# A residual block's 3x3 convolutions, from two output rows at a time to four

## Chip, cores and metric

The program runs on one core of one Trainium2 chip. The metric is the device time of one execution in microseconds (us), the median of several runs. A core has TensorE (PE, matrix products into PSUM), VectorE (DVE), ScalarE (ACT), GpSimd (POOL) and SyncE (SP, which here only issues DMA transfers). Each engine takes its instructions in its own order; semaphores tie the engines together.

## What is computed

An image tensor x of shape 2 x 128 x 128 x 128 (batch B, channels, rows H, columns), float32, runs through four layers. Layers 0 and 2 are a 3x3 convolution with a small state-space scan over eight tokens, group norm and SiLU; layer 1 scales by a coarse gate. The change is in layer 3, a residual block with binarised weights:

```python
w1b = w1 + lax.stop_gradient(jnp.sign(w1) - w1)
w2b = w2 + lax.stop_gradient(jnp.sign(w2) - w2)
out = jax.nn.relu(_batchnorm(_conv3x3(x, w1b), gamma1, beta1))
out = _batchnorm(_conv3x3(out, w2b), gamma2, beta2)
out = out + x
return jax.nn.relu(out)
```

Batch norm takes mean and variance over batch, rows and columns, so the second convolution starts only when the first is complete.

## The kernel before

Channels lie on the 128 partitions. Layers 0 to 2 take the program to about 6937 us. The function `_basic_block` is layer 3. Its whole result Y (2 x 128 rows of 128 columns, 128 KiB a partition) stays in SBUF; the block works in 32 bands of `BAND` = 8 rows, 16 to an image.

Both convolutions use a Winograd form along the rows: a pair of output rows is had from four input rows. Four combinations of input rows (the four lines of `combine`, L855, on POOL) are each multiplied by one of four combinations of the three weight rows (`u`, made once at the start, L817 to L827), for the three columns of the kernel (`kw`), so that a band of four pairs takes 4 x 3 = 12 matmuls of 512 columns (L862) into a PSUM tile `m` of four banks. There are two such tiles. ACT copies one product to SBUF (L870), DVE makes the even and odd rows from the four products by four additions (L873 to L876), and two `bn_stats` (L878) take the band's statistics.

`convolve` runs over the bands with `tc.manual_schedule`, so each engine keeps the order in which the code is written: in step k the load of band k+3, the making of band k+2, the combinations of band k+1, and matmuls and emptying (`conv`) of band k. In the first convolution `load` (L915, L917) fetches y and the residual, `residual` applies group norm and SiLU on ACT (L923), adds the residual on POOL (L924) and stores the band to x3 in DRAM (L925). In the second `normalised` copies two rows from the band before on POOL (L936) and applies batch norm and ReLU on ACT (L938). Three band buffers and two buffers for the combinations turn round. After the second convolution a last loop (L949 to L952) loads x3, adds, applies ReLU and stores the output.

Of the kernel before, what the change touches and what calls it, by code (L numbers as in the profile page):

```python
# [24 lines left out]
F32 = mybir.dt.float32  # L25
U8 = mybir.dt.uint8
AF = mybir.ActivationFunctionType
ALU = mybir.AluOpType
# [3 lines left out]
P = 128  # L32
# [10 lines left out]
BAND = 8  # L43
# [748 lines left out]
                        stage(*order[n - lag])  # L792


def _basic_block(tc, src, y, norm, x3, w1, w2, bn, out, B, H):

    nc = tc.nc  # L800
    pairs = BAND // 2
    with tc.tile_pool(name="bb", bufs=1) as cp, tc.tile_pool(name="bband", bufs=2) as bp, tc.tile_pool(
        name="ps_c", bufs=2, space=PSUM
    ) as pp:

        def combined():
            return bp.tile([P, 4, pairs, P + 2], F32, tag="comb", name="comb")

        bnc = cp.tile([P, 4], F32, tag="bnc", name="bnc")
        nc.sync.dma_start(out=bnc, in_=bn)  # L810
        ws = []
        for n, wd in enumerate((w1, w2)):
            room = [combined().rearrange("p a b c -> p (a b c)")[:, : 9 * P] for _ in range(2)]
            wt, sg = room
            nc.sync.dma_start(out=wt, in_=wd)
            nc.scalar.activation(sg, wt, AF.Sign)
            nc.vector.tensor_tensor(sg, sg, wt, ALU.subtract)  # L817
            nc.vector.tensor_tensor(wt, wt, sg, ALU.add)

            u = cp.tile([P, 4, 3, P], F32, tag=f"u{n}", name=f"u{n}")  # L820
            g = wt.rearrange("p (k t c) -> p k t c", k=3, t=3)
            half = sg.rearrange("p (k t c) -> p k t c", k=3, t=3)
            nc.vector.tensor_copy(u[:, 0:4:3], g[:, 0:3:2])
            nc.vector.tensor_tensor(half[:, 0], g[:, 0], g[:, 2], ALU.add)
            nc.vector.tensor_tensor(u[:, 1], half[:, 0], g[:, 1], ALU.add)
            nc.vector.tensor_tensor(u[:, 2], half[:, 0], g[:, 1], ALU.subtract)
            nc.vector.tensor_scalar_mul(u[:, 1:3], u[:, 1:3], 0.5)  # L827
            ws.append(u)
        Y = cp.tile([P, B, H, P], F32, tag="Y", name="Y")

        room = []
        for n in range(3):
            room.append(cp.tile([P, BAND + 2, P + 2], F32, tag=f"band{n}", name="band"))
            nc.gpsimd.memset(room[n][:, :, 0 : P + 2 : P + 1], 0.0)
        bands = [(b, r0) for b in range(B) for r0 in range(0, H, BAND)]

        def span(k):

            r0 = bands[k][1]
            return room[k % 3], 1 if r0 == 0 else 0, BAND + 1 if r0 + BAND == H else BAND + 2  # L840

        def border(k):
            xb, lo, hi = span(k)
            if lo == 1:
                nc.gpsimd.memset(xb[:, 0, :], 0.0)
            if hi == BAND + 1:
                nc.gpsimd.memset(xb[:, BAND + 1, :], 0.0)

        def combine(k):

            xb = span(k)[0]
            v = combined()
            d = [xb[:, n : n + BAND - 1 : 2, :] for n in range(4)]
            for i, (m, n, op) in enumerate(((0, 2, ALU.subtract), (1, 2, ALU.add), (2, 1, ALU.subtract), (1, 3, ALU.subtract))):
                nc.gpsimd.tensor_tensor(v[:, i], d[m], d[n], op)  # L855
            return v

        def conv(u, v, b, r0, stats):
            m = pp.tile([P, 4, pairs, P], F32, tag="m", name="m")
            for i in (1, 2, 0, 3):  # L860
                for kw in range(3):
                    nc.tensor.matmul(  # L862
                        m[:, i],
                        lhsT=u[:, i, kw, :],
                        rhs=v[:, i, :, kw : kw + P],
                        start=(kw == 0),
                        stop=(kw == 2),
                    )
            m1 = bp.tile([P, pairs, P], F32, tag="m1", name="m1")
            nc.scalar.copy(m1, m[:, 1])  # L870
            rows = Y[:, b, r0 : r0 + BAND, :]
            y0, y1 = rows[:, 0:BAND:2, :], rows[:, 1:BAND:2, :]
            nc.vector.tensor_tensor(y0, m1, m[:, 2], ALU.add)  # L873
            nc.vector.tensor_tensor(y1, m1, m[:, 2], ALU.subtract)
            nc.vector.tensor_tensor(y0, y0, m[:, 0], ALU.add)
            nc.vector.tensor_tensor(y1, y1, m[:, 3], ALU.subtract)  # L876
            for n in range(BAND // ROWS):
                nc.vector.bn_stats(  # L878
                    stats[:, (b * H + r0) // ROWS + n, :],
                    rows[:, n * ROWS : (n + 1) * ROWS, :].rearrange("p r w -> p (r w)"),  # L880
                )

        def affine(stats, n):
            mv = cp.tile([P, 2], F32, tag=f"mv{n}", name="mv")
            nc.vector.bn_aggr(mv, stats.rearrange("p a b -> p (a b)"))
            rstd = _rstd(nc, cp, mv[:, 1:2], BN_EPS, f"bn{n}")
            return _affine(nc, cp, mv[:, 0:1], rstd, bnc[:, 2 * n : 2 * n + 1], bnc[:, 2 * n + 1 : 2 * n + 2], f"bn{n}")

        def rest():
            return bp.tile([P, BAND + 2, P], F32, tag="xs", name="xs")  # L890

        def convolve(u, load, make, n):

            stats = cp.tile([P, B * H // ROWS, 6], F32, tag="st", name="st")
            v = {}
            E = mybir.EngineType
            with tc.manual_schedule(engines={E.PE, E.Activation, E.DVE, E.Pool, E.SP}):
                for k in range(-3, len(bands)):
                    for ahead, f in ((3, load), (2, make)):
                        if 0 <= k + ahead < len(bands):  # L900
                            f(k + ahead)
                    if 0 <= k + 1 < len(bands):
                        v[k + 1] = combine(k + 1)
                    if k >= 0:
                        conv(u, v.pop(k), *bands[k], stats)
            return affine(stats, n)

        rests = {}

        def load(k):  # L910
            b, r0 = bands[k]
            xb, lo, hi = span(k)
            rows = slice(r0 - 1 + lo, r0 - 1 + hi)
            border(k)
            nc.sync.dma_start(out=xb[:, lo:hi, 1 : P + 1], in_=y[b][:, rows, :])  # L915
            rests[k] = rest()[:, lo:hi, :]
            nc.sync.dma_start(out=rests[k], in_=src[b][:, rows, :])  # L917

        def residual(k):
            b, r0 = bands[k]  # L920
            xb, lo, hi = span(k)
            x = xb[:, lo:hi, 1 : P + 1]
            nc.scalar.activation(x, x, AF.Silu, bias=norm[b][1], scale=norm[b][0])  # L923
            nc.gpsimd.tensor_tensor(x, x, rests.pop(k), ALU.add)  # L924
            nc.sync.dma_start(out=x3[b][:, r0 : r0 + BAND, :], in_=xb[:, 1 : BAND + 1, 1 : P + 1])  # L925

        s1, t1 = convolve(ws[0], load, residual, 0)

        def normalised(k):
            b, r0 = bands[k]
            hb, lo, hi = span(k)
            border(k)
            if lo == 0:
                nc.gpsimd.tensor_copy(hb[:, 0:2, 1 : P + 1], span(k - 1)[0][:, BAND : BAND + 2, 1 : P + 1])  # L936
                lo = 2
            nc.scalar.activation(  # L938
                hb[:, lo:hi, 1 : P + 1], Y[:, b, r0 + lo - 1 : r0 + hi - 1, :], AF.Relu, bias=t1, scale=s1
            )  # L940

        s2, t2 = convolve(ws[1], lambda k: None, normalised, 1)

        for k, (b, r0) in enumerate(bands):
            if k % 2 == 0:
                xr = rest()[:, :BAND, :]
            else:
                xr = combined().rearrange("p a b c -> p (a b c)")[:, : BAND * P].rearrange("p (r w) -> p r w", r=BAND)
            nc.sync.dma_start(out=xr, in_=x3[b][:, r0 : r0 + BAND, :])  # L949
            nc.vector.scalar_tensor_tensor(xr, Y[:, b, r0 : r0 + BAND, :], s2, xr, ALU.mult, ALU.add)  # L950
            nc.scalar.activation(xr, xr, AF.Relu, bias=t2)
            nc.scalar.dma_start(out=out[b, :, r0 : r0 + BAND, :], in_=xr)  # L952
# [3 lines left out]
def _program(ctx, tc, d, cols, out):  # L956
    nc = tc.nc
    B, _, H, _ = d["x"].shape
# [5 lines left out]
    with tc.tile_pool(name="const", bufs=1) as cp, tc.tile_pool(name="wts", bufs=1) as wp:  # L964
# [4 lines left out]
        w1 = cp.tile([P, CG], F32, tag="w1", name="w1")  # L969
# [18 lines left out]
        w, stats = layer(x2, 2)  # L988
        with tc.tile_pool(name="ps_n", bufs=1, space=PSUM) as pp:
            norm = [_norm(nc, npool, pp, w, con, stats, b) for b in range(B)]  # L990
    _basic_block(tc, x2, y, norm, x3, d["L3_w1"], d["L3_w2"], d["L3_bn"], out, B, H)


def _host_layout(inputs):
# [40 lines left out]
```

## Time and profile before

| | us |
|---|---|
| median of 3 runs | 7748.62 (7738.88 to 7761.49) |
| span of the profiled run | 7761.8 |
| block begins (first load of its weights) | 6937.5 |
| first convolution, first to last matmul | 6970.5 to 7302.4 |
| second convolution, first to last matmul | 7315.1 to 7647.0 |
| last loop, to the end | 7647.0 to 7761.8 |

A profile page lists, for one execution, the busy time of each engine, groups of equal instructions by source line with count, mean duration and the idle time of the engine just before them (with what ended it), and the chain of work that ended last. A timeline gives the start and length of each instruction, and a table by stage the busy time of each engine in a stretch of time with the TensorE clock granted in it (1.00 is full speed). One float32 matmul appears as two matmul records, each with a weight load (PEld) of its own. The end of a matmul is modelled, so records that follow each other overlap. Of the whole span DVE is busy 6759.3 us and PE 6470.4 us; the earlier layers make up most of both.

### The profile page before, as it was taken

What the parts mean: (1) busy time and instruction counts of PE and PEld (TensorE: products, weight loads), DVE (VectorE), ACT (ScalarE), POOL (GpSimd) and SP (SyncE); (2) the same over time, 40 slices, a digit from 0 to 9 for tenths busy, and PEclk for the clock granted to TensorE, in tenths of its full rate; (3) what the DMA queues carried; (4) which work ended last, traced back from release to release, by engine and by line L of the source; (5) the groups of instructions that cost most, each with busy time, mean ns of one, the idle gap of its engine ahead of it and who ended that gap; (6) DMA issues with size and microseconds to landing.
All of it is one profiled execution on the core that took longest, in us unless ns stands there. A gap on an engine that the chain in (4) does not pass through costs nothing.

```text
span 7761.8 us, 87240 instructions
## 1 busy us (share of the span) xinstructions
PE 6470.4 (83%) x29648; PEld 2196.5 (28%) x29648; DVE 6759.3 (87%) x6304; ACT 4272.3 (55%) x4873; POOL 5628.0 (73%) x1879
## 2 busy tenths in 40 slices
PE   7888888888888888867888888888888888869994
PEld 2222222222222222243222222222222222224441
DVE  5999999999999999965999999999999999983333
ACT  4666665665666666554566565665666666631112
POOL 5777877877877778742777777777777777767541
PEclk8999999999999999877999999999999999979997
DMA  7999999999999999954999999999999999975204
GB/s 194 248 252 247 254 245 247 249 251 250 253 244 254 248 247 253 240 185 137 238 249 250 247 247 246 253 252 244 250 253 247 252 246 251 250 202 173 93 0 168
DMA packets 573438, 1767.29 MB, mean 228 GB/s; under 512 B 85536, under 2 KB 239680, under 8 KB 458176
## 3 DMA queue, kind: packets, MB, share of 16 engines
q1 hardware_dynamic: 568384, 1744.92, 86.3%
q10 hardware_dynamic: 4608, 16.78, 0.5%
q8 instruction: 236, 3.87, 0.2%
q14 instruction: 210, 1.72, 0.1%
HBM read 1551.65 MB, written 209.72 MB: 227 GB/s over the span
## 4 chain that ended last, share of the span: by engine, by line
DVE 35%; DMA 31%; PE 19%; issue 6%; POOL 4%; ACT 4%; SPq 2%; POOLq 0%; DVEq 0%; ACTq 0%
DMA bcr<-sb 24%; DVE set L471 12%; DVE h L476 10%; DVE r L472 10%; PE m L862 9%; DMA ur<-su 3%; POOL h L444 3%; PE one L348 2%; PE set L453 2%; ACT set L462 1%; PE one L399 1%; PE ys L491 1%; DVE v L504 1%; PE ys L482 1%; DMA band<-in_x_dram 1%
## 5 line engine op out<-in xcount | busy, mean ns | idle before, releaser
L444 POOL TENSOR_TENSOR h<-ur,bcr 128x2048 f32<-128x2048 f32 x896 | 4059.3, 4537 | 1282.1 <-DMA bcr<-sb 1063.4
L471 DVE TENSOR_TENSOR set<-set,h 128x1024 f32<-128x1024 f32 x1792 | 2192.2, 1223 | 297.3 <-ACT set L462 291.8
L472 DVE TENSOR_TENSOR r<-set,bcr 128x1024 f32<-128x1024 f32 x1792 | 2193.8, 1224 | 61.4
L462 ACT ACTIVATE set<-set 128x1024 f32<-128x1024 f32 x1792 | 1745.2, 1007 | 843.2 <-PE set L453 828.6
L476 DVE TENSOR_TENSOR h<-set,h 128x1024 f32<-128x1024 f32 x1536 | 1862.7, 1213 | 38.8 <-POOL h L444 38.3
L453 PE MATMUL set<-dt,rep 32*128 32x512 f32 x7168 | 1402.4, 674 | 95.9 <-DVE h L476 90.3
L491 PE MATMUL ys<-r,ct 128*32 128x512 f32 x7168 | 1165.6, 633 | 32.2 <-DVE r L472 32.0
L321 PE MATMUL one<-band,conv 128*128 128x512 f32 x2304 | 1086.6, 608 | 23.3 <-DMA band<-in_x_dram 12.6
L399 PE MATMUL one<-xc,keep 128*64 128x512 f32 x1024 | 319.6, 707 | 476.4 <-ACT xc L356 361.4
L862 PE MATMUL m<-comb,u 128*128 128x512 f32 x1536 | 663.8, 595 | 38.7 <-POOL comb L855 38.7
L453 PEld LDWEIGHTS set<-dt,rep 32*128 32x128 f32 x7168 | 407.4, 193 | 988.3 <-issue 468.3
L321 PEld LDWEIGHTS one<-band,conv 128*128 128x128 f32 x2304 | 408.7, 190 | 674.1 <-issue 599.5
L482 PE MATMUL ys<-t,ct 128*128 128x512 f32 x512 | 325.4, 722 | 251.3 <-DVE v L504 249.8
L350 ACT ACTIVATE xc<-one,keep 128x512 f32<-128x512 f32 x256 | 176.0, 687 | 516.6 <-PE one L348 511.9
L491 PEld LDWEIGHTS ys<-r,ct 128*32 128x32 f32 x7168 | 182.5, 111 | 916.4 <-issue 755.3
L873 DVE TENSOR_TENSOR Y<-m,m 128x512 f32<-128x512 f32 x64 | 43.9, 687 | 436.2 <-ACT m L870 436.2
L855 POOL TENSOR_TENSOR comb<-band 128x520 f32<-128x520 f32 x256 | 298.2, 1198 | 162.4 <-PE m L862 160.4
L419 PE MATMUL one<-prod,ct 128*128 128x512 f32 x512 | 290.9, 651 | 144.6 <-POOL prod L411 115.1
L862 PEld LDWEIGHTS m<-comb,u 128*128 128x128 f32 x1536 | 291.8, 190 | 410.0 <-issue 363.4
L348 PE MATMUL one<-y,w_in 128*128 128x512 f32 x512 | 342.7, 757 | 5.8 <-ACT xc L350 3.1
L870 ACT COPY m<-m 128x512 f32<-128x512 f32 x64 | 37.5, 586 | 556.8 <-issue 474.7
L373 POOL TENSOR_TENSOR u<-dt,xc 128x1024 f32<-128x1024 f32 x128 | 302.5, 2363 | 46.1 <-ACT dt L367 45.9
(126 smaller groups left out, 6263.8 us busy)
## 6 DMA issues: line engine op xcount, KB each, us to landing
ur<-su SPq DMA_DIRECT2D x896, 896.0 KB, 11.6
bcr<-sb SPq DMA_DIRECT2D x896, 448.0 KB, 11.8
ur<-su SPq DMA_DIRECT2D x896, 128.0 KB, 11.2
su<-u SPq DMA_DIRECT2D x1024, 64.0 KB, 2.9
sb<-bc SPq DMA_DIRECT2D x256, 224.0 KB, 2.8
bcr<-sb SPq DMA_DIRECT2D x896, 64.0 KB, 11.1
y<-o SPq DMA_DIRECT2D x128, 256.0 KB, 9.2
band<-in_x_dram SPq DMA_DIRECT2D x28, 640.0 KB, 11.0
```

Of the source, the lines that this page charges most:

```text
L321: nc.tensor.matmul(py.rearrange("p (r w) -> p r w", r=ROWS), lhsT=w["conv"][:, tap, :], rhs=xb[:, r + kh : r + kh + ROWS, kw : kw + P], st ...
L348: nc.tensor.matmul(p, lhsT=w[("in", "z")[i]][:, g, :], rhs=s["y"], start=True, stop=True)
L399: nc.tensor.matmul(p[g * NQ * DS : (g + 1) * NQ * DS, :], lhsT=w[("xb", "xcm")[i]], rhs=s["xc"][:, g, :], start=True, stop=True,)
L444: nc.gpsimd.tensor_tensor(b, s["ur", t], s["bc", t][:, 0].unsqueeze(1).to_broadcast([P, NJ, NS]), ALU.mult)
L453: nc.tensor.matmul(a[j // 2][:, j % 2, :], lhsT=w["rep"][r, q, :], rhs=s["dt"][r, g, :], start=True, stop=True, tile_position=(r.start, 0),)
L462: nc.scalar.activation(x, x, AF.Exp)
L471: nc.vector.tensor_tensor(pt, pt, s["h", t - 1][:, js, :], ALU.mult)
L472: nc.vector.tensor_tensor(s["r", t][:, js, :], pt, s["bc", t - 1][:, 1].unsqueeze(1).to_broadcast([P, 2, NS]), ALU.mult)
L476: nc.vector.tensor_tensor(s["h", t][:, js, :], pt, s["h", t][:, js, :], ALU.add)
L482: nc.tensor.matmul(s["ys", g], lhsT=con["ident"], rhs=s["t1"][:, g, :], start=True, stop=False)
L491: nc.tensor.matmul(s["ys", g][a : a + NQ * DJ, :], lhsT=red[:, q, :], rhs=r[:, j, :], start=False, stop=(q == NQ - 1), tile_position=(0, a),)
L862: nc.tensor.matmul(m[:, i], lhsT=u[:, i, kw, :], rhs=v[:, i, :, kw : kw + P], start=(kw == 0), stop=(kw == 2),)
```

## The change

A Winograd form of the next size: four output rows from six input rows, by six combinations. A band of eight rows has two groups of four, so each of its 6 x 3 = 18 matmuls has 256 columns. It is for less TensorE work: 18 x 256 columns a band in place of 12 x 512.

The combinations and the recombination have more steps. `edges` makes part of the six combinations: four scalar-tensor-tensor operations on DVE (for instance row 2 minus four times row 0), then three sums on POOL; `rest_of` finishes them with three more on DVE. `conv` copies two products to SBUF on ACT, forms sums and differences `sd` of two pairs of products, and then the four rows in five operations on DVE. The PSUM tile has three banks, two products to a bank. Step k is now written as: matmuls of band k (`products`), `edges` of k+1, emptying of k (`conv`), `rest_of` k+1.

The six weight combinations take 9 KiB a partition[...]. So that of the second convolution is made at the start in the room of Y's last image, stored to DRAM (`later`) and loaded over the first set between the convolutions.

```diff
-def _basic_block(tc, src, y, norm, x3, w1, w2, bn, out, B, H):
+def _basic_block(tc, src, y, norm, x3, scratch, w1, w2, bn, out, B, H):
...
+        spare = Y[:, B - 1].rearrange("p r w -> p (r w)")[:, : 18 * P].rearrange("p (a t c) -> p a t c", a=6, t=3)
+        for wd, x in ((w1, u), (w2, spare)):
...
+            nc.vector.tensor_scalar_mul(x[:, 0], g[:, 0], 0.25)
+            nc.vector.tensor_copy(x[:, 5], g[:, 2])
+            nc.vector.tensor_tensor(even, g[:, 0], g[:, 2], ALU.add)
+            nc.vector.tensor_tensor(x[:, 3], even, g[:, 1], ALU.add)
+            nc.vector.tensor_tensor(x[:, 2], even, g[:, 1], ALU.subtract)
+            nc.vector.tensor_scalar_mul(x[:, 2:4], x[:, 2:4], -1.0 / 6.0)
...
+            nc.vector.scalar_tensor_tensor(flat[0], flat[4], 4.0, flat[2], ALU.mult, ALU.add)
+            nc.vector.scalar_tensor_tensor(flat[5], flat[3], 2.0, flat[0], ALU.mult, ALU.add)
+            nc.vector.scalar_tensor_tensor(flat[6], flat[3], -2.0, flat[0], ALU.mult, ALU.add)
+            nc.vector.tensor_scalar_mul(x[:, 1:5:3], x[:, 1:5:3], 1.0 / 24.0)
+        later = scratch.tile([P, 18 * P], F32, tag="later", name="later", bufs=1)
+        nc.sync.dma_start(out=later, in_=spare.rearrange("p a t c -> p (a t c)"))
...
-        def combine(k):
+        def edges(k):
             xb = span(k)[0]
             v = combined()
-            d = [xb[:, n : n + BAND - 1 : 2, :] for n in range(4)]
-            for i, (m, n, op) in enumerate(((0, 2, ALU.subtract), (1, 2, ALU.add), (2, 1, ALU.subtract), (1, 3, ALU.subtract))):
-                nc.gpsimd.tensor_tensor(v[:, i], d[m], d[n], op)
+            low, high = [xb[:, n : n + BAND, :].rearrange("p (i n) w -> p n i w", n=4) for n in (0, 2)]
+            for n, at in enumerate((0, 3, 2, 5)):
+                nc.vector.scalar_tensor_tensor(v[:, at], low[:, n], -4.0, high[:, n], ALU.mult, ALU.add)
+            nc.gpsimd.tensor_tensor(v[:, 1:5:3], high[:, 1:3], low[:, 1:3], ALU.subtract)
+            nc.gpsimd.tensor_tensor(v[:, 0:6:5], v[:, 2:6:3], v[:, 0:4:3], ALU.subtract)
+            nc.gpsimd.tensor_tensor(v[:, 3], v[:, 2], v[:, 3], ALU.add)
             return v
...
+        def rest_of(v):
+            x = [v[:, n].rearrange("p i w -> p (i w)") for n in range(6)]
+            nc.vector.scalar_tensor_tensor(x[4], x[1], -2.0, x[4], ALU.mult, ALU.add)
+            nc.vector.scalar_tensor_tensor(x[1], x[1], 4.0, x[4], ALU.mult, ALU.add)
+            nc.vector.scalar_tensor_tensor(x[2], x[2], 2.0, x[3], ALU.mult, ALU.subtract)
...
-            m = pp.tile([P, 4, pairs, P], F32, tag="m", name="m")
-            for i in (1, 2, 0, 3):
+        def products(v):
+            m = pp.tile([P, 3, 2, fours, P], F32, tag="m", name="m")
+            for n, i in enumerate((2, 4, 3, 1, 0, 5)):
                 for kw in range(3):
                     nc.tensor.matmul(
-                        m[:, i],
+                        m[:, n // 2, n % 2],
...
-            m1 = bp.tile([P, pairs, P], F32, tag="m1", name="m1")
-            nc.scalar.copy(m1, m[:, 1])
+        def conv(m, b, r0, stats):
+            c = bp.tile([P, 2, fours, P], F32, tag="c", name="c")
+            nc.scalar.copy(c, m[:, 0])
+            sd = bp.tile([P, 2, 2, fours, P], F32, tag="sd", name="sd", bufs=1)
+            nc.vector.tensor_tensor(sd[:, :, 0], m[:, 1], c, ALU.add)
+            nc.vector.tensor_tensor(sd[:, :, 1], m[:, 1], c, ALU.subtract)
             rows = Y[:, b, r0 : r0 + BAND, :]
-            y0, y1 = rows[:, 0:BAND:2, :], rows[:, 1:BAND:2, :]
-            nc.vector.tensor_tensor(y0, m1, m[:, 2], ALU.add)
-            nc.vector.tensor_tensor(y1, m1, m[:, 2], ALU.subtract)
-            nc.vector.tensor_tensor(y0, y0, m[:, 0], ALU.add)
-            nc.vector.tensor_tensor(y1, y1, m[:, 3], ALU.subtract)
+            y = rows.rearrange("p (i n) w -> p n i w", n=4)
+            (s1, d1), (s2, d2) = [(sd[:, n, 0], sd[:, n, 1]) for n in range(2)]
+            nc.vector.tensor_tensor(y[:, 0:4:3], m[:, 2], sd[:, 0], ALU.add)
+            nc.vector.scalar_tensor_tensor(y[:, 1], d2, 2.0, d1, ALU.mult, ALU.add)
+            nc.vector.scalar_tensor_tensor(y[:, 2], s2, 4.0, s1, ALU.mult, ALU.add)
+            nc.vector.tensor_tensor(y[:, 0], y[:, 0], s2, ALU.add)
+            nc.vector.scalar_tensor_tensor(y[:, 3], d2, 8.0, y[:, 3], ALU.mult, ALU.add)
...
+                    if k >= 0:
+                        m = products(v.pop(k))
                     if 0 <= k + 1 < len(bands):
-                        v[k + 1] = combine(k + 1)
+                        v[k + 1] = edges(k + 1)
                     if k >= 0:
-                        conv(u, v.pop(k), *bands[k], stats)
+                        conv(m, *bands[k], stats)
+                    if 0 <= k + 1 < len(bands):
+                        rest_of(v[k + 1])
...
+        nc.sync.dma_start(out=u.rearrange("p a t c -> p (a t c)"), in_=later)
+        s2, t2 = convolve(lambda k: None, normalised, 1)
```

## The prediction

> **What bounds the kernel now.** The table by stage comes first: the basic block is the end of the program, from 6937 us. Its two convolutions fill 6970.5 to 7302.4 and 7315.1 to 7647.0 us; the 115 us after them are a DMA-bound tail that the change leaves alone. Columns: window, length, then busy us of PE, PE weight loads, DVE, ACT, POOL with counts, granted clock, DMA share, GB/s.
>
> ```profile
> 7100.00:7200.00 100.00, 100.00 (x234) 44.04 (x233) 34.76 (x56) 17.79 (x20) 70.97 (x51) 1.00 0.54 171
> 7450.00:7550.00 100.00, 100.00 (x235) 44.04 (x234) 37.66 (x60) 17.26 (x20) 49.81 (x50) 1.00 0.00 0
> ```
>
> PE never stops, at full clock; DVE is busy a third of the time, POOL 50 to 71%. The page's groups agree:
>
> ```profile
> L862 PE MATMUL m<-comb,u 128*128 128x512 f32 x1536 | 663.8, 595 | 38.7 <-POOL comb L855 38.7
> L855 POOL TENSOR_TENSOR comb<-band 128x520 f32<-128x520 f32 x256 | 298.2, 1198 | 162.4 <-PE m L862 160.4
> L873 DVE TENSOR_TENSOR Y<-m,m 128x512 f32<-128x512 f32 x64 | 43.9, 687 | 436.2 <-ACT m L870 436.2
> ```
>
> PE waited 38.7 us in all, POOL and DVE waited for PE. The 768 matmuls give 1536 records, two each. The timeline of one band:
>
> ```profile
> 7189.15 0.58 ACT L870 COPY m<-m 128x512 f32<-128x512 f32 x1 [8.36 <-issue]
> 7189.64 1.46 ACT L923 ACTIVATE band<-band,aff_t,aff_s 128x1280 f32<-128x1280 f32 x1
> ...
> 7189.77 0.69 DVE L873 TENSOR_TENSOR Y<-m,m 128x512 f32<-128x512 f32 x1 [6.50 <-ACT m L870]
> ...
> 7191.17 2.68 POOL L924 TENSOR_TENSOR band<-band,xs 128x1280 f32<-128x1280 f32 x1 [3.02 <-ACT band L923]
> ...
> 7192.29 1.29 DVE L878 BATCH_NORM_STATS2 st<-Y 128x6 f32<-128x512 f32 x2
> ...
> 7199.45 0.58 ACT L870 COPY m<-m 128x512 f32<-128x512 f32 x1 [8.36 <-issue]
> ```
>
> The period is 7199.45 - 7189.15 = 10.30 us, 24 records of 0.429 us. ACT's copy reads the first quarter of the products, yet:
>
> ```profile
> 7639.58 7.46 PE L862 MATMUL m<-comb,u 128*128 128x512 f32 x17
> ...
> 7647.12 0.58 ACT L870 COPY m<-m 128x512 f32<-128x512 f32 x1 [9.71 <-PE m L862]
> ```
>
> PE ends at 7647.04 and the copy starts 0.08 us later: the emptying of a band waits for its last matmul. That costs nothing here, as PE is on the next band, whose combinations POOL made ahead.
>
> [...]
>
> ```profile
> 6958.99 2.97 POOL L924 TENSOR_TENSOR band<-band,xs 128x1152 f32<-128x1152 f32 x1 [8.47 <-DMA xs<-x]
> 6959.74 3.43 DVE L818 TENSOR_TENSOR comb<-comb 128x1152 f32<-128x1152 f32 x1
> ```
>
> L818 alone takes 1.34 us; here it ends 1.21 us after POOL's end at 6961.96. L873 to L876 have a PSUM input and keep 0.68 us beside POOL. [...] (last but two numbers: POOL and clock):
>
> ```profile
> 7304.00:7306.00 2.00, 0.00 (x0) 0.00 (x0) 1.97 (x4) 0.34 (x1) 0.00 (x0) 0.92 0.00 0
> 7306.00:7308.00 2.00, 0.00 (x0) 0.00 (x0) 1.97 (x3) 0.00 (x0) 0.00 (x0) 0.50 0.00 0
> ...
> 7316.00:7318.00 2.00, 2.00 (x4) 0.87 (x3) 0.00 (x0) 0.00 (x0) 2.00 (x4) 0.50 0.00 0
> 7318.00:7320.00 2.00, 2.00 (x5) 0.82 (x4) 0.00 (x0) 0.00 (x0) 2.00 (x3) 0.67 0.00 0
> 7320.00:7322.00 2.00, 2.00 (x7) 0.80 (x6) 0.00 (x0) 0.00 (x0) 2.00 (x2) 1.00 0.00 0
> ```
>
> PE stopped at 7302.4, halved near 7305.7, restarted at 7315.08 and was whole again near 7319.3. [...] L862's full-array pairs go at 0.429 us[...] and
>
> ```profile
> 6938.16 2.05 PE L511 MATMUL po<-keep,v 128*128 128x128 f32 x16 [0.48 <-DVE v L504]
> ```
>
> gives (2.05 - 0.275) / 15 = 0.118 us a record with its weight load. Weight loads are hidden at 256 columns too.
>
> **The change, part by part.** *PE:* 12 matmuls of 512 columns become 18 of 256, 36 records of about 0.215 us: 7.74 us a band for 10.30 (ceiling 0.225, 8.1 us). First start to last end is 35 x 0.215 + 0.378 = 7.90 us (a record outlasts its issue by 0.595 - 0.429). Alone that would save 64 x 2.56 = 164 us.
>
> *DVE and POOL, throughput:* POOL falls from 4.65 to two 520-element sums of 1.2 and a 260-element one of about 0.65, 3.05 us. DVE's scalar-tensor-tensor is L950, whose back-to-back starts lie 1.19 us apart at 1024 elements (7656.66, 7657.85): 0.125 + N/0.96, so 0.39 us for 256 or 260. A tensor-tensor steps 0.60 at 512, about 0.34 at 256. Four edges 1.58, two sums to sd 1.32, five to Y 2.63, statistics 1.2, three in rest_of 1.32: about 8 us for 4. It would fit under 10.3; it isn't the point.
>
> *The order, the point:* DVE takes its instructions in order, and rest_of(k+1) stands behind conv(k). In the built program PE raises its semaphore once, by 18, at the last of a band's matmuls; the copy in conv(k) waits for that, and the first matmul of band k+1 (combination 2) waits for the last instruction of rest_of(k+1). So products(k), conv(k), rest_of(k+1), products(k+1) run one after the other, and the two PSUM buffers overlap nothing. Behind the waiting first sd sum on DVE stand its twin, five sums to Y, two statistics and rest_of's three, and PE waits for all. From PE's start: products 7.90; to the copy 0.08; copy and handover 0.62; sd 0.60 + 0.72; first sum to Y 0.60; two at 0.39; one at 0.34; the last with its wait 0.52; statistics 1.20; rest_of 0.53 + 0.40 + 0.49; to PE 0.06. Sum 14.8 us. The edges and POOL's sums of k+1 (1.58 + 1.2 + 0.65 = 3.4 us after rest_of) hide under the products; so do loads, stores and SiLU.
>
> *Port, first convolution:* SiLU follows the copy at once as at 7189.64, so the residual sum holds POOL from 2.02 to 4.70 us after the copy's start (7191.17 - 7189.15, and 2.68). DVE reaches its first sum with two SBUF inputs at 2.54 and is held to 4.70: 2.16 us. POOL's next instruction, the difference for k+1, is ready at once and costs up to 1.2 more: 3.4 us[...]. In the second convolution that difference runs under the sd sums, whose PSUM input keeps them free: 0.
>
> *Clock:* PE now idles 7 us (10 in the first convolution) each band, long enough to halve the clock. It restarted at half clock for 3.9 us (6970.5) and 4.2 us (7315.08), losing half of that; [...]I take 3.6 us, a loss of 1.8 (0 to 2.15).
>
> *Periods:* 14.8 + 1.8 + 3.4 = 20.0 us and 14.8 + 1.8 = 16.6 us, for 10.30. 32 x (20.0 + 16.6) = 1171 us for 331.9 + 332.0 = 664: +507 us.
>
> *Once each:* w2's preparation stands ahead of band 0's edges on DVE; after 6963.17 it has about 8 us for 5.1, then edges, POOL and rest_of 4.7 for POOL's 2.3, and w2's DMA starts later with the longer preparation of w1: about +7. Between the convolutions, 12.7 us today, the longer emptying and the edges add 3.5; the end +1.1. The store of w2's weights hides behind residual and first bands. The reload of 1.18 MB at the stage's 170 GB/s takes 7 us from the last matmul and hides in those 16 us. Sum +12. In all 7748.6 + 507 + 12 = 8268 us.
>
> **Rivals.** *Overlap after all:* if rest_of(k+1) did not hold PE, DVE's 8 us would pace it: 64 x 8.4 = 538 us, with +12 gives 7635 us. For it speaks that DVE and POOL have the idle time; against it the single semaphore and the FIFO. 4%. *Serial, no port loss:* scalar-tensor-tensor isn't seen beside POOL in this trace: 32 x 33.2 = 1062, so 8159 us; 13%. *Serial, clock kept:* 32 x (18.2 + 14.8) = 1056, so 8153 us, or 8115 with the smaller port loss; against it the halving above; 13%. *Neither:* 32 x 29.6 = 947, so 8044 us; 5%. *All ceilings:* +0.4 PE, +0.35 clock: 1219, so 8316 us; 5%. My case has 60%.
>
> **Numbers.** Predicted 8268 us. From 8100 to 8330 the range holds my case with both port values (8230 to 8268), both one-loss rivals and the ceilings; outside lie overlap and the loss-free chain. Every serial case is slower: 0.95; overlap 0.04; 0.01 between.
>
> **What would show it.** PE about half busy in both convolutions, its waits put down to DVE comb; DVE's Y sums waiting for the ACT copy; the first scalar-tensor-tensor after the sd sums about 2.5 us long in the first convolution and 0.5 in the second; clock 0.5 at each band's start; starts of the copies 20 and 16.6 us apart. A PE that runs through from band to band would refute the whole.

## The result, and the profile after

The changed kernel takes 8282.31 us (median of 4 runs, 8272.81 to 8296.91), the kernel before 7743.75 us (7736.28 to 7761.49): 1.069 times as long (95% interval 1.0668 to 1.0712). The predicted 8268 us is 14 us short.

In the two profiled runs the block goes from its first weight load to the end in 7761.8 - 6937.45 = 824.3 us before and 8276.1 - 6921.10 = 1355.0 us after. The stages:

| stage of the block, us | before | after | difference | predicted |
|---|---|---|---|---|
| first weight load to first matmul | 33.1 | 39.9 | +6.8 | +7 |
| first convolution, first to last matmul | 331.9 | 637.5 | +305.6 | +308 |
| between the convolutions | 12.7 | 16.6 | +3.9 | +3.5 |
| second convolution, first to last matmul | 332.0 | 540.0 | +208.0 | +199 |
| last matmul to the end | 114.8 | 121.1 | +6.3 | +1.1 |
| sum | 824.3 | 1355.0 | +530.7 | +519 |

The earlier layers took 16.3 us less in this run than in that of before; the change does not touch them.

The table by stage of the kernel after, in the two stretches shown of before. Columns as there: busy us of PE, PE weight loads, DVE, ACT and POOL with counts, then clock, DMA share and GB/s.

```profile
7100.00:7200.00 100.00, 53.69 (x180) 43.46 (x180) 48.35 (x78) 9.69 (x10) 29.01 (x20) 0.75 0.27 87
7700.00:7800.00 100.00, 62.52 (x216) 50.66 (x216) 40.01 (x92) 10.36 (x12) 21.86 (x24) 0.80 0.00 0
```

PE was busy all of it before. Now it is busy 54% and 63%, at a mean clock of 0.75 and 0.80, and no other engine is busy more than half of the time. The page's groups of the kernel after say what each waits for:

```profile
L881 PE MATMUL m<-comb,u 128*128 128x256 f32 x2304 | 676.8, 466 | 550.0 <-DVE comb L874 550.0
...
L892 ACT COPY c<-m 128x512 f32<-128x512 f32 x64 | 37.5, 585 | 1082.9 <-issue 948.8
L894 DVE TENSOR_TENSOR sd<-m,c 128x512 f32<-128x512 f32 x64 | 44.3, 692 | 644.3 <-ACT c L892 644.3
```

L881 answers to L862 and L894 to L873 of before. PE waited 38.7 us before and waits 550.0 us now, all of it for L874, the last instruction of `rest_of`. DVE in turn waits 644.3 us for the copy, and the copy for PE. Each waits for the other: a closed ring. Nor is PE's busy time smaller, although 18 x 256 columns a band are 25% fewer than 12 x 512: 676.8 us for 663.8, because part of it now runs at a granted clock of 0.50 (steps below). POOL's three sums (L865 to L867) take 217.7 us for the 298.2 of L855. The timeline of one band of the first convolution:

```profile
7256.71 0.58 ACT L892 COPY c<-m 128x512 f32<-128x512 f32 x1 [18.53 <-issue]
...
7258.73 2.66 POOL L955 TENSOR_TENSOR band<-band,xs 128x1280 f32<-128x1280 f32 x1 [9.73 <-ACT band L954]
7259.26 2.41 DVE L900 SCALAR_TENSOR_TENSOR Y<-sd 128x256 f32<-128x256 f32 x1
7261.35 1.47 POOL L865 TENSOR_TENSOR comb<-band 128x520 f32<-128x520 f32 x1
7261.60 1.50 DVE L901 SCALAR_TENSOR_TENSOR Y<-sd 128x256 f32<-128x256 f32 x1
7263.02 0.41 DVE L902 TENSOR_TENSOR Y<-Y,sd 128x256 f32<-128x256 f32 x1
...
7266.37 10.88 PE L881 MATMUL m<-comb,u 128*128 128x256 f32 x36 [9.74 <-DVE comb L874]
...
7277.33 0.58 ACT L892 COPY c<-m 128x512 f32<-128x512 f32 x1 [18.68 <-issue]
```

and of one of the second:

```profile
7916.10 0.58 ACT L892 COPY c<-m 128x512 f32<-128x512 f32 x1 [15.34 <-issue]
7916.10 1.29 POOL L865 TENSOR_TENSOR comb<-band 128x520 f32<-128x520 f32 x1 [6.78 <-PE m L881]
...
7918.65 0.42 DVE L900 SCALAR_TENSOR_TENSOR Y<-sd 128x256 f32<-128x256 f32 x1
...
7922.67 10.42 PE L881 MATMUL m<-comb,u 128*128 128x256 f32 x36 [6.65 <-DVE comb L874]
...
7933.16 0.58 ACT L892 COPY c<-m 128x512 f32<-128x512 f32 x1 [15.34 <-issue]
```

Copy, emptying, `rest_of`, the 36 matmul records, the next copy: of this chain nothing of one band lies beside the next; only `edges`, loads and stores run under the products. From the copy to PE's start it is 7266.37 - 7256.71 = 9.66 us in the first convolution and 6.57 us in the second. The 3.09 us between are two instructions: L900 takes 2.41 us beside POOL's residual sum L955 and L901 1.50 us beside L865, where both take 0.42 us in the second convolution, whose L865 has run out by then. What the prediction and the expectations call the port is seen here as such longer times beside POOL and as nothing else; what in the chip causes them was not shown.

The products take 10.88 and 10.42 us; they take 8.01 in e5 below, at clock 1.00, and in e1. The clock in half-microsecond steps of the second convolution (last but two number):

```profile
7920.00:7920.50 0.50, 0.00 (x0) 0.00 (x0) 0.47 (x2) 0.00 (x0) 0.00 (x0) 1.00 0.00 0
7920.50:7921.00 0.50, 0.00 (x0) 0.00 (x0) 0.50 (x2) 0.00 (x0) 0.00 (x0) 0.72 0.00 0
7921.00:7921.50 0.50, 0.00 (x0) 0.00 (x0) 0.50 (x2) 0.00 (x0) 0.00 (x0) 0.50 0.00 0
...
7927.00:7927.50 0.50, 0.50 (x3) 0.35 (x2) 0.00 (x0) 0.00 (x0) 0.00 (x0) 0.50 0.00 0
7927.50:7928.00 0.50, 0.50 (x4) 0.45 (x3) 0.00 (x0) 0.00 (x0) 0.00 (x0) 0.96 0.00 0
...
7937.50:7938.00 0.50, 0.00 (x0) 0.00 (x0) 0.50 (x2) 0.00 (x0) 0.00 (x0) 0.78 0.00 0
```

A mean of 0.72 between 1 and 0.5 puts the fall at 7920.72, one of 0.96 the rise at 7927.54, one of 0.78 the next fall at 7937.78. So it is 6.82 us at half clock in a cycle of 17.06 us, and PE, which restarts at 7922.67, has 4.87 us of it, a loss of 2.4 us.

The periods are remarkable. The starts of the copies lie 20.48 us apart in most bands of the first convolution (20.62 in the one shown, where one image ends and the next begins) and 17.07 us in the second. These are 6 x 3.413 and 5 x 3.413 us, and the half-clock spell, 6.82 us, is 2 x 3.41. Whether that is chance became a question for the experiments.

### The profile page after: what moved, and what is told of

It is laid out like the page before. It is cut to its first block, busy times and chain, and to the rows that moved or that the text cites. A ratio compares the mean times of both kernels' runs of the same rounds, so it can differ in the third digit from the quotient of the medians.

```text
span 8276.1 us, 89343 instructions
## 1 busy us (share of the span) xinstructions
PE 6485.5 (78%) x30416; PEld 2448.7 (30%) x30416; DVE 7072.5 (85%) x6954; ACT 4272.5 (52%) x4873; POOL 5546.4 (67%) x1815
## 4 chain that ended last, share of the span: by engine, by line
DVE 34%; DMA 29%; issue 16%; PE 11%; ACT 4%; POOL 4%; SPq 2%; POOLq 0%; DVEq 0%; ACTq 0%
DMA bcr<-sb 22%; DVE set L471 11%; DVE h L476 10%; DVE r L472 9%; DMA ur<-su 4%; POOL h L444 3%; PE set L453 2%; PE one L348 2%; ACT set L462 1%; PE one L399 1%; PE ys L491 1%; DVE v L504 1%; PE m L881 1%; PE ys L482 1%; PE one L321 1%
## 5 line engine op out<-in xcount | busy, mean ns | idle before, releaser
L881 PE MATMUL m<-comb,u 128*128 128x256 f32 x2304 | 676.8, 466 | 550.0 <-DVE comb L874 550.0
L321 PE MATMUL one<-band,conv 128*128 128x512 f32 x2304 | 1086.1, 608 | 23.4 <-DMA band<-in_x_dram 12.6
L881 PEld LDWEIGHTS m<-comb,u 128*128 128x128 f32 x2304 | 547.8, 241 | 678.6 <-issue 563.5
L892 ACT COPY c<-m 128x512 f32<-128x512 f32 x64 | 37.5, 585 | 1082.9 <-issue 948.8
L894 DVE TENSOR_TENSOR sd<-m,c 128x512 f32<-128x512 f32 x64 | 44.3, 692 | 644.3 <-ACT c L892 644.3
```

The costliest lines, as they stand in the source:

```text
L321: nc.tensor.matmul(py.rearrange("p (r w) -> p r w", r=ROWS), lhsT=w["conv"][:, tap, :], rhs=xb[:, r + kh : r + kh + ROWS, kw : kw + P], st ...
L881: nc.tensor.matmul(m[:, n // 2, n % 2], lhsT=u[:, i, kw, :], rhs=v[:, i, :, kw : kw + P], start=(kw == 0), stop=(kw == 2),)
```

## Experiments

The theory: one ring (products, emptying, `rest_of`, products) sets the time, since `rest_of` stands behind the emptying on DVE, and two losses lie on the ring: in the first convolution DVE instructions that take longer beside a sum of POOL (L900 2.41 us and L901 1.50 us, for 0.42 in the second), and the clock in both. The rivals: that the order costs little and the work itself (more DVE steps, smaller matmuls) is too slow; that the clock is the cause and not a consequence; that the long DVE instructions have another cause than POOL. The kernel before took 7746.6 us beside e1 to e4, 7754.25 beside e5 to e8 and 7742.15 beside e9. A period is the distance between the starts of successive copies (`nc.scalar.copy` in `conv`). e1 to e7 are one run each, e8 and e9 medians of four. The kernels compute the same output; e4 computes one sum twice and e5 adds products that nothing reads.

**e1: `rest_of` ahead of the emptying.**

```diff
-                    if k >= 0:
-                        conv(m, *bands[k], stats)
                     if 0 <= k + 1 < len(bands):
                         rest_of(v[k + 1])
+                    if k >= 0:
+                        conv(m, *bands[k], stats)
```

> Only the order is changed: rest_of(k+1) stands ahead of conv(k). Serial theory: products(k+1) no longer wait for conv(k). After the end of a band's products DVE still has conv (5.2 us from the copy), edges 1.4, the wait for POOL's two sums 2.1 and rest_of's last 0.5 before the band after next: about 9.3 us between bands in the second convolution, for 17.1, at full clock. The first keeps the loss at the port (3.1): 12.4, or up to 13.7 with half clock. In all about 7800 us (7760 to 7850). Rival, that the time is the greater amount of DVE work or dearer small matmuls: no change in these amounts, so about 8280 us.

Measured: 7792.0 us. Two moved lines give back 490 of the 539 us. The second convolution goes at 8.93 us a band, under the 10.30 of before; the timeline there:

```profile
7568.32 0.59 DVE L874 SCALAR_TENSOR_TENSOR comb<-comb 128x260 f32<-128x260 f32 x1 [0.63 <-POOL comb L867]
...
7569.06 8.01 PE L881 MATMUL m<-comb,u 128*128 128x256 f32 x36 [0.92 <-DVE comb L874]
```

PE takes 8.01 us for the 36 records, as e5 does at clock 1.00, and waits 0.92 us for a chain of POOL and DVE. The first convolution does not run evenly: its periods are 7.77 us and 15.5 to 18.4 us in turn, 12.4 on average, because the residual sum meets L900 and L901 in one band, as in the kernel after, and `rest_of` in the next (read from the timeline; no run tests it by itself):

```profile
7216.13 2.65 POOL L955 TENSOR_TENSOR band<-band,xs 128x1280 f32<-128x1280 f32 x1
7216.20 2.87 DVE L874 SCALAR_TENSOR_TENSOR comb<-comb 128x260 f32<-128x260 f32 x1 [0.62 <-POOL comb L867]
```

So the order is the cause of nearly all, and the steps and small matmuls are no obstacle in themselves; but with this order alone the kernel is still slower than before.

**e2: the residual sum later on POOL.** `make(k + 2)` is written after `edges(k + 1)`, so that the residual sum stands behind POOL's sums for `edges` and is done under the products.

```diff
-                    for ahead, f in ((3, load), (2, make)):
-                        if 0 <= k + ahead < len(bands):
-                            f(k + ahead)
+                    if 0 <= k + 3 < len(bands):
+                        load(k + 3)
...
                         v[k + 1] = edges(k + 1)
+                    if 0 <= k + 2 < len(bands):
+                        make(k + 2)
```

> The residual sum on POOL stands behind POOL's sums for band k+1, so that it runs while DVE waits for the products. Port theory: in the first convolution the two first sums of Y with both inputs in SBUF fall from 2.4 and 1.5 us to 0.42, the period from 20.5 to that of the second, 17.1: 32 x 3.4 = 110 us less, about 8175 us. Rival, that the first convolution is longer for its loads and stores or for SiLU: period stays near 20.5, about 8280 us.

Measured: 8183.6 us; both convolutions at 17.07 us. In the first, by the timeline:

```profile
7268.55 0.41 DVE L900 SCALAR_TENSOR_TENSOR Y<-sd 128x256 f32<-128x256 f32 x1
...
7272.56 7.61 PE L881 MATMUL m<-comb,u 128*128 128x256 f32 x23 [6.65 <-DVE comb L874]
```

L900 is down from 2.41 to 0.41 us and PE's wait from 9.74 to 6.65, the 3.09 us; the period falls by 3.41, one step of 3.413. The cause of the long instructions is POOL's residual sum beside them: moved in time, it costs them nothing. 98.7 us of the loss are put down to it, the clock's part in that step included.

**e3: a PSUM tile for each of the three pairs of products**, so that the copy waits for 12 records instead of 36.

```diff
-            m = pp.tile([P, 3, 2, fours, P], F32, tag="m", name="m")
+            m = [pp.tile([P, 2, fours, P], F32, tag=f"m{n}", name="m") for n in range(3)]
...
-                        m[:, n // 2, n % 2],
+                        m[n // 2][:, n % 2],
```

> The PSUM tile is three tiles of a bank each, so copy and sd sums start when their own products are done. Theory of the end-of-band semaphore: copy and sd sums (0.62 + 1.32) move under the products, 1.9 us off the chain, and SiLU and residual sum with them, so the port loss goes too. [...]13.65 us in both convolutions, 8282 - 32 x (20.5 - 13.65) - 32 x (17.07 - 13.65) = about 7955 us. Without that step: 12.6 us and a loss of 1 to 2.5, any period from 13.6 to 15.1, 7950 to 8050 us. If the semaphore is not what holds the copy: 8280 us.

Measured: 8080.1 us. The period is not 13.65 us (4 x 3.413): it is 15.89 and 14.83 in turn, in both convolutions, 15.36 on average, and the pair is 30.72 = 9 x 3.413. In the first convolution:

```profile
7216.20 9.55 PE L881 MATMUL m<-comb,u 128*128 128x256 f32 x36 [5.25 <-DVE comb L874]
...
7222.67 2.68 POOL L955 TENSOR_TENSOR band<-band,xs 128x1280 f32<-128x1280 f32 x1 [3.08 <-ACT band L954]
7223.27 0.69 DVE L894 TENSOR_TENSOR sd<-m,c 128x512 f32<-128x512 f32 x1 [5.86 <-PE m L881]
...
7225.79 0.69 DVE L899 TENSOR_TENSOR Y<-m,sd 128x512 f32<-128x512 f32 x1 [1.23 <-PE m L881]
7226.40 1.00 DVE L900 SCALAR_TENSOR_TENSOR Y<-sd 128x256 f32<-128x256 f32 x1
```

The copy and the sd sums now lie under the products, and PE's wait shrinks to 5.25 us, by 1.40 in the second convolution. In the first it shrinks more, because the residual sum, released by the earlier copy, is over before L900 comes. This confirms that one semaphore for the whole tile held the emptying back; it is a fifth of the wait, since `rest_of` still stands behind the rest. The miss has two parts. L900 now meets L865 in both convolutions (1.00 us for 0.42), so that without the clock's loss the ring would be 8.01 + 5.25 = 13.26 us and not the 12.6 expected; and a period of 13.65 us would leave the clock 0.39 us, where 2.1 us were lost on average. The clock is taken up below.

**e4: one sum twice**, 0.7 us more on DVE and on the ring in every band.

```diff
             nc.vector.tensor_tensor(sd[:, :, 1], m[:, 1], c, ALU.subtract)
+            nc.vector.tensor_tensor(sd[:, :, 1], m[:, 1], c, ALU.subtract)
```

> The second sd sum is made twice (same result): 0.6 us more on the serial chain of each band. If the chain and the clock loss simply add up: 64 x 0.6 = 38 us more, or 19 where half of it falls away, about 8300 to 8320 us, periods of about 17.4 to 17.7 and 20.8 to 21.1. [...]periods stay at 17.07 and 20.48 us and the time within 5 us of 8282, the added work being paid for by a shorter stretch at half clock.

Measured: 8287.3 us, against 8282.3, and periods of 20.48 and 17.07 us again. 64 x 0.7 us of work on the ring cost nothing that can be measured: the two convolutions take 637.7 and 539.4 us from first to last matmul, for 637.5 and 540.0. The second convolution:

```profile
7911.66 0.69 DVE L896 TENSOR_TENSOR sd<-m,c 128x512 f32<-128x512 f32 x1
...
7917.02 9.69 PE L881 MATMUL m<-comb,u 128*128 128x256 f32 x36 [7.37 <-DVE comb L874]
...
7926.79 0.59 ACT L892 COPY c<-m 128x512 f32<-128x512 f32 x1 [15.34 <-issue]
```

PE's wait is 0.72 us longer than after's 6.65 and its products are 0.73 us shorter than the 10.42. The later start had less of the half-clock spell left, and wait and products together are 17.06 us for 17.07. The ring came to five times 3.413 us by degrees; the first periods of this second convolution are 17.18, 17.17, 17.12, 17.09, 17.08, 17.07.

**e5: e2, and PE kept busy.** 13 matmuls into a PSUM tile that is not read follow each band's products.

```diff
+            f = fp.tile([P, 2, P], F32, tag="fill", name="fill")
+            for n in range(13):
+                nc.tensor.matmul(f, lhsT=u[:, 0, 0, :], rhs=u[:, 5, 0:2, :], start=(n == 0), stop=(n == 12))
             return m
```

> The residual sum stands late, as in the run before with that edit, and after each band's products TensorE makes 13 further matmuls of 256 columns into a bank of its own that nobody reads (5.6 us, shorter than the gap of 6.6). Clock theory: the clock stays at 1.00, the products take 7.9 us in place of 10.4, and the period is the bare chain, 7.9 + 6.6 = 14.5 us in both convolutions: 32 x 2 x (17.07 - 14.5) = 164 us less than with the late residual alone, about 8020 us (8010 to 8030). If the clock costs nothing: 8184 us or more.

Measured: 8044.3 us, 139 us less than e2 with 64 x 5.6 us more work for PE; 14.66 us in both convolutions, no longer a multiple of 3.413. That is 14 us above the range expected: the ring is 14.66 and not 14.5, and the earlier layers, which the edit does not touch, took 10.6 us more than in e2 (the block begins at 6938.4 for 6927.8). The timeline, then the table by stage:

```profile
7251.39 5.77 PE L890 MATMUL fill<-u 128*128 128x256 f32 x26
...
7258.20 8.01 PE L881 MATMUL m<-comb,u 128*128 128x256 f32 x36 [1.04 <-DVE comb L874]
```

```profile
7000.00:7400.00 400.00, 371.99 (x1696) 318.59 (x1695) 191.76 (x434) 53.98 (x56) 162.53 (x113) 1.00 0.41 125
```

At clock 1.00 the products take 8.01 us for 10.42. The clock is a consequence of the ring's idle time, not the cause of it: without the waits for POOL and the clock's loss the ring alone is 14.66 us, still 4.4 more than before's 10.30.

**e6: the emptying one band later.** `conv(k - 1)` stands where `conv(k)` was, with `rest_of(k + 1)` behind it.

```diff
-                    if k >= 0:
-                        conv(m, *bands[k], stats)
+                    if k >= 1:
+                        conv(m.pop(k - 1), *bands[k - 1], stats)
```

> conv of band k-1, in place of k, stands between edges and rest_of of band k+1; two PSUM tiles and two buffers for the combinations as before. Serial theory: nobody waits for products just issued; DVE's 7.1 us a band and about 1.1 us at the port with POOL's first sum make 8.3 us in the second convolution, and the residual sum on POOL makes about 10.5 in the first: 32 x 18.8 = 602 us for the 664 of the kernel before, and about 14 us of longer start and middle: 7700 us (7670 to 7760). If half clock or the port still rule: no gain on the run with rest_of first, 7790 us.

Measured: 7772.5 us, more than the expected 7700. The ring is open, and every second band takes 7.8 to 8.4 us in the first convolution and 7.77 in the second, but the ones between take mostly 12.3 to 14 and 10.15 or 11.84. In the second:

```profile
7509.60 2.55 DVE L864 SCALAR_TENSOR_TENSOR comb<-band 128x260 f32<-128x260 f32 x4 [0.72 <-PE m L881]
7509.65 0.59 ACT L892 COPY c<-m 128x512 f32<-128x512 f32 x1 [8.42 <-issue]
7509.65 1.53 POOL L865 TENSOR_TENSOR comb<-band 128x520 f32<-128x520 f32 x1 [4.17 <-PE m L881]
```

`edges` waits for PE: with two buffers for the combinations, those of band k+1 go where band k-1's were and must wait for its products. Released together, DVE's L864 and POOL's L865 also run beside each other, and L864 takes 2.55 us for 1.44. The expectation had overlooked this second wait.

**e7: e6, and the residual sum on DVE.**

```diff
-            nc.gpsimd.tensor_tensor(x, x, rests.pop(k), ALU.add)
+            nc.vector.tensor_tensor(x, x, rests.pop(k), ALU.add)
```

`make(k + 2)` is also written after the emptying, so that DVE does not wait for ACT.

> As the kernel that empties a band later, with the residual sum on DVE (1.4 us for POOL's 2.7), behind conv in each step. Port theory: [...]DVE's work rises to 8.5: about 9.7 us in the first convolution and 8.3 in the second, 7670 us (7640 to 7720). If DVE's own work is the bound instead: slower than with the sum on POOL, by up to 32 x 1.4 = 45 us.

Measured: 7733.8 us, above the 7640 to 7720 expected; periods of 7.77 and 12.72 us in the first convolution, and still 7.77 with 10.24 or 11.93 in the second. The residual sum takes 1.48 us on DVE for 2.66 on POOL. The alternation stays: it is not from POOL's residual sum.

**e8: e7, and three buffers for the combinations.**

```diff
-            return bp.tile([P, 6, fours, P + 2], F32, tag="comb", name="comb")
+            return bp.tile([P, 6, fours, P + 2], F32, tag="comb", name="comb", bufs=3)
```

> As the kernel with the residual sum on DVE, with three buffers for the combinations, so that edges and POOL's first sum need not wait for the products two bands back. TensorE's 7.75 us paces the second convolution at about 7.9, DVE's 8.5 the first at about 8.7: 32 x 16.6 = 531 us for 664, and 14 us once: 7630 us (7610 to 7680), 1.5% below the kernel before. If the collisions at the port remain as they are with two buffers: 7670 us.

Measured: 7665.7 us (7645.9 to 7679.4), 0.9884 of before (0.9863 to 0.9904). The alternation is gone, 9.65 and 8.58 us in nearly every band, so it came from the buffers. Not all of the gain on e7 lies in the convolutions: from the last matmul to the end it is 108.9 us for e7's 121.4; the last loop loads into the same buffers. What is left over 7.8 us are DVE instructions beside POOL's L865 and, in the first convolution, DVE's own work, about 8.5 us a band (an estimate: 9.65 less 0.96 that L873 and 0.21 that L900 lose beside POOL):

```profile
7210.45 1.34 POOL L865 TENSOR_TENSOR comb<-band 128x520 f32<-128x520 f32 x1 [4.14 <-DVE band L957]
7210.68 1.39 DVE L873 SCALAR_TENSOR_TENSOR comb<-comb 128x260 f32<-128x260 f32 x1
...
7484.15 1.35 POOL L865 TENSOR_TENSOR comb<-band 128x520 f32<-128x520 f32 x1
7484.27 1.51 DVE L902 TENSOR_TENSOR Y<-Y,sd 128x256 f32<-128x256 f32 x1
```

**e9: e8, with these meetings moved.** The residual sum stands ahead of the statistics, so that L865 runs beside these (1.27 us for the two at 7107.40, 1.29 without L865 at 7202.28); in the second convolution L865 is done by DVE.

```diff
-            nc.gpsimd.tensor_tensor(v[:, 1:5:3], high[:, 1:3], low[:, 1:3], ALU.subtract)
+            (nc.vector if n else nc.gpsimd).tensor_tensor(v[:, 1:5:3], high[:, 1:3], low[:, 1:3], ALU.subtract)
...
+                    if 0 <= k + 2 < len(bands):
+                        make(k + 2)
+                    if k >= 1:
+                        stats_of(*bands[k - 1], stats)
```

> As the kernel with three buffers and the residual sum on DVE, with the two collisions left in its trace moved: in the first convolution the residual sum stands ahead of the statistics, so that POOL's first sum for the next band runs under bn_stats, which has one SBUF input, and not against rest_of; in the second that sum (520 elements) is made by DVE itself. Port theory: the first convolution's period falls from 9.65 by 1.0 to about 8.65 us, the second's from 8.58 by 1.1 and up by 0.6 to about 8.1: 32 x 1.5 = 48 us less, about 7618 us (7600 to 7640). If the 1.4 to 1.5 us of those two instructions are not collisions: no gain in the first, 0.6 us more in the second, 7685 us.

Measured: 7599.0 us (7590.2 to 7618.8), 0.9827 of before (0.9794 to 0.9860), just under the range expected; 8.75 us a band in the first convolution, 7.88 in the second. From the first weight load to the end it is 7588.3 - 6899.64 = 688.7 us in the profiled run, 135.6 less than before and 49 less than e8 (7664.9 - 6927.23 = 737.7); the rest of the difference between e8 and e9 lies in the earlier layers of the runs. The table by stage over its two convolutions:

```profile
6934.50:7213.40 278.90, 257.90 (x1152) 216.81 (x1152) 269.54 (x526) 57.10 (x60) 103.57 (x96) 0.99 0.64 196
7230.00:7481.70 251.70, 251.67 (x1151) 216.39 (x1149) 241.17 (x524) 51.18 (x60) 88.44 (x94) 1.00 0.02 5
```

In the second convolution PE is busy 251.67 of 251.70 us: it sets the time again, with 25% fewer columns, and the form's saving is there (332.0 - 252.6 = 79 us from first to last matmul), though DVE is close behind at 96%. In the first DVE is busy 97% and sets the time. This is the fastest of all, 1.7% below the kernel before.

## Why the prediction was right

**The order and the single semaphore: right.** PE waits 550.0 us for L874, DVE 644.3 us for the copy, and the copy starts 0.08 us after the last matmul. e1 shows it by moving two lines (490 us back), e3 by the semaphore (PE's wait 6.65 to 5.25 us). The rival "overlap after all" was priced at 7635 us for DVE alone setting the pace; e1 and e6 show that it takes more than opening the ring: with a third buffer and the residual sum off POOL e8 came to 7666, and with two such meetings of DVE and POOL moved e9 to 7599. The rival's 8 us of DVE work a band were too many as well. The second convolution has 7.1: 5.72 from the first sd sum to the last of `rest_of` (7916.72 to 7922.44) and 1.36 for `edges`. The 2.63 us put down for the five to Y is more than its own terms, 0.60 + 3 x 0.39 + 0.34 = 2.11.

**PE: right.** 36 records take 8.01 us from first start to last end in e1 and, at clock 1.00, in e5, for the 7.90 worked out; bands that follow each other without a wait start 7.77 us apart (e6), for 7.74. The weight loads, one to a record, are hidden in these times.

**The DVE chain: 0.3 us too long.** From the copy to PE's start 6.57 us were measured, 6.86 predicted. A scalar-tensor-tensor of 256 elements follows the one before after 0.33 us (7918.65 to 7918.98), not after the 0.39 scaled down from 1024 elements. The 0.96 elements a nanosecond of that scaling are in the trace of before (1.36 us for 1152 elements at L817, 0.56 for 384 at L824: 768 elements in 0.80 us); its fixed part, 0.125 us, was too large for these.

**The wait for POOL: right in kind, 0.3 us too large.** 3.09 us for 3.4: L900 lost 2.00 beside the residual sum (2.16 predicted), L901 1.09 beside POOL's next sum (1.2 predicted). The prediction's 8230 us counts L900's part alone. e2 takes it away by time alone. The rival without it stood at 8159 us; e2 came to 8184.

**The clock: right in kind, size too small, by more than the range given.** Against the 8.01 us of full clock the loss was 2.4 us in the second convolution (10.42) and 2.7 in the first (PE is busy 342.89 us over 32 bands, 10.72 each), for 1.8 with a ceiling of 2.15. The step that failed is the reading of 3.9 and 4.2 us after two restarts as if they were the spread. (The first was itself 4.1: the clock of 0.71 between 6974 and 6975 puts the rise at 6974.58.) In the kernel after, PE restarted at 7922.67 and had 4.87 us at half clock before the rise at 7927.54; in the cheaper bands of e3, which lost 1.54 (8.01 to 9.55), it was 3.12 us (7216.20 to 7219.32, last section). So the time ran from 3.1 to 4.9 us, and two restarts did not give its spread. An estimate of the most: PE at work through the whole half-clock spell of 6.82 us would lose half of it, 3.4 us.

**The periods.** With the measured terms, 8.01 + 0.08 + 6.57 = 14.66 us for the bare ring (14.8 predicted; e5 has 14.66), plus 2.41 is 17.07; with 3.09 and 2.71 in place of 2.41 it is 20.46: the periods measured are 17.07 and 20.48, those predicted 16.6 and 20.0. The ring and the wait for POOL were too large by 0.15 and 0.3, the clock too small by 0.6 and 0.9, so each period is short by less than half a microsecond. That the errors offset each other was luck.

**The sums.** 32 whole periods for a convolution count the wait behind the last band, which is not in the stretch from first to last matmul, and the last two periods of the first convolution are only 17.3 and 17.2, with no residual left to make. So 640 predicted stand against 637.5 measured, and 531 against 540.0; the shortfall of the periods was partly hidden by counting one too many. The costs outside were +6.8, +3.9 and +6.3 for +7, +3.5 and +1.1. The reload of the weights was issued at 7598.48, just when PE stopped, and landed in 5.1 us (7 predicted), long before PE's restart at 7615.00: hidden, as said. Of the last +6.3, 0.85 is the longer emptying and its way to the first sum of the last loop (9.20 for 8.35 us); the other 5.5 lie in that loop, which waits for its transfers in both kernels (DVE 60.9 us before L950, 63.3 us before L982 of after). Their cause was not looked for.

**Rivals in one row.** The chain without both losses was priced at 8044 us, and e5, which is this case, took 8044.3; the agreement is closer than the terms, of which the bare ring was 14.8 for 14.66, and so in part luck.

## What to carry to other kernels

When a loop is written as one order for all engines, follow one iteration round: if the instructions that feed the next iteration's matmuls stand behind the emptying of this one on the same in-order engine, double buffers overlap nothing, and fewer columns for PE only made it wait here, 550.0 us at a mean clock of 0.75 and 0.80. Opening this ring paid off clearly only with three changes together: the emptying a step later, a buffer more for what is now made ahead, and DVE instructions that take longer beside POOL's sums (0.42 us became up to 2.87) moved away from these. Whether a third buffer with `rest_of` first (the order of e1) would do as well was not tried. A saving in the engine that sets the time is had only if the chain that takes its place is shorter than the new time of that engine.

## What was not expected of the hardware

**A ring that idled PE fell into step with the changes of the clock.** After's 20.48 and 17.07 us, e2's 17.07 and e4's 20.48 and 17.07 are all multiples of 3.413 us (a sixth of 20.48), and e3's two bands together are 9 of them. The 3.413 us do not come from the ring: in the trace of before, which has none, the clock rose at 6974.58, fell at 7305.68 and rose at 7319.32 by the same working, 331.10 and 13.64 us apart, which is 97 and 4 x 3.413. What sets them was not shown. With the ring in step, 0.7 us more a band was free (e4), while 3.09 us less gave 3.41 (e2). An estimate fits all: with a loss of 1.5 us (the least measured, in e3) to 3.4 (the estimate from the 6.82 us) the products take 9.5 to 11.4 us. PE's wait of 6.65 us (after, e2) then allows a period of 16.2 to 18.1, which holds 17.07; 7.37 (e4) allows 16.9 to 18.8, and 9.74 allows 19.2 to 21.1, which holds 20.48. With e3's 5.25 it is 14.8 to 16.7, which holds no multiple, neither 13.65 nor 17.07, and the ring alternates over two bands instead. The cheap one of these two is the line of e3 shown above, where PE restarts at 7216.20. The clock around it:

```profile
7215.50:7216.00 0.50, 0.00 (x0) 0.00 (x0) 0.50 (x3) 0.00 (x0) 0.00 (x0) 0.91 0.00 0
...
7219.00:7219.50 0.50, 0.50 (x3) 0.41 (x2) 0.00 (x0) 0.00 (x0) 0.50 (x1) 0.68 0.62 150
```

It fell at 7215.91 and rose at 7219.32, 3.41 us later; PE was idle for the first 0.29 us of it. That the periods would stay was expected before e4 ran; the range that explains e3 was worked out after the runs, and none was made to test it alone.

**Short DVE instructions took as long as POOL's sums beside them.** A scalar-tensor-tensor of 0.42 us with both inputs in SBUF took 2.41, 2.87 or 1.50 us beside a sum of POOL that had started 0.07 to 0.53 us before it, and ended 0.28 or 0.29 us after that sum. The trace of before had shown such times for a tensor-tensor and a copy (L823, 2.92 us beside L924 for 0.56), not for a scalar-tensor-tensor. POOL's next sum, L865, started at 7261.35, before L901 did at 7261.60: one long POOL queue caught DVE twice in a row.
